# A deformable convolution's last three groups: two vertical taps per matmul; and a third x buffer in the wkv layer

## The chip, the cores and the metric

The kernel runs on one core of a Trainium2 chip. The metric is the time of one execution on the device in microseconds (us); lower is better. The core has five engines with their own instruction queues: PE (TensorE, matmuls, with its weight loads as PEld), DVE (VectorE), ACT (ScalarE), POOL (GpSimd) and SP (SyncE, which here only issues DMA transfers). They meet through semaphores.

## What is computed

Four residual layers on x, an array of (2, 192, 96, 96) floats, each on a group-normalised copy: layer 0 is a pair of deformable convolutions, layer 1 a 1 x 1 convolution with edge features, layer 2 a two-way RWKV recurrence ("wkv"), layer 3 a state space model. The change touches layers 0 and 2. All arithmetic is in 32-bit floats.

```python
# layer 0: twice (width and height branch), G = 10 groups of 18 channels, 9 taps
patches = val.reshape(Bx, C, KK, Hx, Wx)      # bilinear samples at learned offsets
out = jnp.einsum('bikhw,oik->bohw', patches, weight.reshape(Cout, Cin, KK))
# layer 2: per channel, forward and backward over the 9216 positions
no = jnp.maximum(o, u + kt); A = jnp.exp(o - no); Bw = jnp.exp(u + kt - no)
y = (A * p + Bw * vt) / (A * q + Bw)
no2 = jnp.maximum(w + o, kt)
A2 = jnp.exp(w + o - no2); B2 = jnp.exp(kt - no2)
carry = (A2 * p + B2 * vt, A2 * q + B2, no2)
```

## The kernel before

**Layer 0, near0 (L473 on).** It runs once for each of the two images; while image 0 runs, `reduce0` prepares image 1 in between (matmuls at L302, loads of `xt` at L285). An image has 79 tiles: 72 of 8 x 16 positions in 12 strips of six, and 7 on the right and lower edge. A tile passes three stages l = 0, 1, 2, each for up to four groups of channels. In a stage PE transposes the interpolation weights `sp` (L587; copied out by ACT L595 and DVE L593 as `st`), and `sample` multiplies them with the windows `xw` (L634). ACT copies the samples to `val` (L655). POOL makes the hats `h` (L541) and loads `xw` (L559), DVE the products `sp` (L571).

`gathered` (L661 on) then moves `val` with SP's DMAs, group by group, 18 lanes each, into two tiles that are laid out by channel: `main` for the first seven groups (126 lanes, both branches behind one another; L672, 14 transfers a tile) and `more` for groups 7, 8 and 9 (54 lanes from lane 0 for one branch, 54 from lane 64 for the other; L679, 12 transfers a tile). `val` has three buffers per half, `main` and `more` two.

`convolve` (L683 on) multiplies by the weights: for each of 3 blocks of 64 output channels, each of 9 taps and each branch (`cv`) one matmul, added into `pf` in PSUM at a place that is shifted by the tap. The two branches use different columns of PE. It is a generator in three parts, 26, 28 and 54 matmuls: `main` in two halves, then `more`. They run during the next tile's stages 0, 1 and 2, each after that stage's `sample`. At the end of a chunk of three tiles DVE adds `pf` to the row buffer `fa`, and every six tiles `done` writes a strip. PE, ACT and DVE keep the program's order here; POOL and SP are ordered by the scheduler. SP also reads the offsets `raw` (L504) three tiles ahead, writes `u_d` (L520), and in image 0 loads `xt`.

**Layer 2 (L1499 on).** 18 chunks of 512 positions by 3 lane groups, first forward, then backward: 108 steps, software pipelined by the loop at its end. `load(i + 6)` reads x for a new chunk (`xt`, L1661, two buffers), `key` and `value` or `gate` multiply it on PE (all L1605), `top` scans on DVE (L1716), `weighted` makes four exponentials on ACT, each in two instructions (L1731, L1733): `b`, `a`, `eb`, `ea`. `a` and `ea` of the backward half share two PSUM buffers called `e`. `sums` runs two scans (L1755) and two products on DVE; `own`, `ended`, `crossed` and `added` are on POOL; `logged` (L1800, L1801) makes a reciprocal `r` on ACT for `scaled` on DVE (L1813 on). `tail` normalises a chunk and writes it out (L1827 to L1893). All but SP keep the program's order.

Of the kernel before, what the change touches and what calls it, by code (L numbers as in the profile page):

```python
# [6 lines left out]
F32 = mybir.dt.float32  # L7
# [11 lines left out]
P = 128  # L19
CH = 96  # L20
CM, MH = 180, 90
G, CG, KK = 10, 18, 9
# [8 lines left out]
PS = 4  # L31
# [3 lines left out]
LT = P  # L35
# [3 lines left out]
XW = 104  # L39
OB, OA = 97, 291  # L40
MAIN = 7
CO = 64
NO = 3
FEW = 4
# [17 lines left out]
class Net:  # L62
# [283 lines left out]
    def near_constants(self, wn, at_d):  # L346

        nc, tc, ins = self.nc, self.tc, self.ins
        con = {}
# [95 lines left out]
        con["one"] = one  # L445

        wd = wn.tile([MAIN * CG, 2, KK, NO * CO], F32, name="wd")
        wl = wn.tile([P, KK, NO * CO], F32, name="wl")
        nc.gpsimd.memset(wl, 0.0)
        nc.gpsimd.memset(wd[:, :, :, CM:], 0.0)  # L450
        for cv in range(2):
            src = ins["w_dcn"][cv].rearrange("(g t c) o -> g c t o", g=G, t=KK)
            for g in range(G):
                at = g * CG if g < MAIN else cv * 64 + (g - MAIN) * CG
                nc.gpsimd.dma_start(
                    out=wd[at : at + CG, cv, :, :CM] if g < MAIN else wl[at : at + CG, :, :CM],
                    in_=src[g],
                )
        con["wd"], con["wl"] = wd, wl

        bo = wn.tile([P, NO], F32, name="bo")
# [13 lines left out]
    def near0(self, b, xp_d, o_d, u_d, f_d, sums, far, top, con, aside=None):  # L475
# [5 lines left out]
        with ExitStack() as ctx:  # L481
# [178 lines left out]
                        )  # L660
                return vals  # L661

            def gathered(main, more, l, vals, nh):

                for e in range(2):
                    val = vals[e].rearrange("p s r c -> p s (r c)")
                    for q in range(2):
                        g = 4 * l + (2 * q if l < 2 else 0) + e
                        for h in range(nh):
                            from_ = slice(h * 64 + q * 32, h * 64 + q * 32 + CG)  # L670
                            if g < MAIN:
                                nc.sync.dma_start(  # L672
                                    out=main[g * CG : (g + 1) * CG, h], in_=val[from_]
                                )
                                continue
                            for cv in range(2) if l < 2 else (q,):
                                lane = cv * 64 + (g - MAIN) * CG
                                s0 = cv * KK if l < 2 else 0
                                nc.sync.dma_start(  # L679
                                    out=more[lane : lane + CG, h], in_=val[from_, s0 : s0 + KK]  # L680
                                )

            def convolve(pf, main, more, kind, e, parts, first, last):  # L683

                nh, rows, columns = parts
                todo = [(m, t) for m in range(NO) for t in range(KK)]
                cut = len(todo) // 2
                for l, part in ((0, todo[:cut]), (0, todo[cut:]), (1, todo)):
                    for m, t in part:
                        ky, kx = 2 - t // 3, 2 - t % 3  # L690
                        y, x = ((ky, 16 * e + kx), (ky, 32 * e + kx), (32 * e + ky, kx))[kind]
                        for cv in range(2):
                            at = slice(cv * 64, cv * 64 + (G - MAIN) * CG) if l else slice(0, MAIN * CG)
                            wt = con["wl"][at, t] if l else con["wd"][:, cv, t]
                            if kind == 1:
                                to = pf[cv * CO : (cv + 1) * CO, m, y : y + rows, x : x + nh * columns]
                                to = to.rearrange("p r (h c) -> p h r c", h=nh)
                            else:
                                to = pf[cv * CO : (cv + 1) * CO, m, y : y + nh * rows, x : x + columns]
                                to = to.rearrange("p (h r) c -> p h r c", h=nh)  # L700
                            took = more[at, :, t] if l else main[:, :, cv * KK + t]
                            nc.tensor.matmul(  # L702
                                to,
                                wt[:, m * CO : (m + 1) * CO],
                                took.rearrange("p h (r c) -> p h r c", c=columns),
                                start=first and l == 0 and t == 0,
                                stop=last and l == 1 and t == KK - 1,
                                skip_group_check=True,
                                tile_position=(at.start, cv * CO),
                            )  # L710
                    yield

            def done(i, fa, ed):

# [28 lines left out]
            fa = s1.tile([P, 3, 10, W + 4], F32, name="fa")  # L743
            nc.gpsimd.memset(fa, 0.0)
            ed = s1.tile([P, 3, H + 4, 4], F32, name="ed")
            nt = STRIPS * 6
            def plan(kind, i, j):

# [104 lines left out]
            for k, (n, l) in enumerate(stages):  # L853
                chunk, e, tile = work[n]
                size, patches = tile[2:]
                kind = chunk[0]
                if l == 0:
                    if n + 1 < len(work):
                        xws[n + 1] = windows(work[n + 1][2][1])
                    where = wheres.get(n + 2, iter(()))  # L860
                    if n + 3 < len(work):
                        wheres[n + 3] = placed(n + 3)
                        next(wheres[n + 3])
                hat = iter(())
                if k + 3 < len(stages):
                    hat = hatted(k + 3)
                    hs[k + 3] = next(hat)
                two = k + 1 < len(stages) and stages[k + 1][1] < 2
                if k + 1 < len(stages):
                    sts[k + 1] = [turn(sps[turned])]  # L870
                    turned += 1
                    if l == 2:
                        next(where, None)
                    make(turned + 1)
                if l == 0:
                    main = sb.tile([MAIN * CG, 2 * KK * LT], F32, name="main")
                    more = sb.tile([P, KK * LT], F32, name="more")
                    parts = split(kind, size, patches)
                    half = parts[1] * parts[2]
                    main, more = (  # L880
                        v[:, : parts[0] * m * half].rearrange("p (h s n) -> p h s n", s=m, n=half)
                        for v, m in ((main, 2 * KK), (more, KK))
                    )
                vals = sample(sts.pop(k), xws[n], l, kind, parts, patches)
                gathered(main, more, l, vals, parts[0])
                next(hat, None)
                next(hat, None)
                next(conv, None)
                if l == 1:
                    next(steps, None)  # L890
                    next(steps, None)
                if two:
                    sts[k + 1].append(turn(sps[turned]))
                    turned += 1
                if l == 0:
                    next(steps, None)
                if l == 1:
                    us[n + 2] = next(where, None)
                if l == 2:
                    next(where, None)  # L900
                    next(conv, None)
                    conv = convolved(n, main, more)
# [592 lines left out]
    def layer2(self, x, out, stats):  # L1495
# [4 lines left out]
        T = 512  # L1500
# [5 lines left out]
        with ExitStack() as ctx:  # L1506
# [3 lines left out]
            s4 = ctx.enter_context(tc.tile_pool(name="l2t", bufs=4))  # L1510
            s1 = ctx.enter_context(tc.tile_pool(name="l2o", bufs=1))
            sy = ctx.enter_context(tc.tile_pool(name="l2y", bufs=2))
            pk = ctx.enter_context(tc.tile_pool(name="l2k", bufs=2, space=PSUM))
            pv = ctx.enter_context(tc.tile_pool(name="l2v", bufs=1, space=PSUM))
            pa = ctx.enter_context(tc.tile_pool(name="l2a", bufs=2, space=PSUM))
# [139 lines left out]
            def load(i):  # L1655
                back, c, g = seq[i]
                if g == 0:
                    xts[back, c] = []
                    for b in range(B):
                        xt = sb.tile([CH, 2, T], F32, name=f"xt{b}")  # L1660
                        nc.sync.dma_start(out=xt, in_=halves(x[b])[:, :, c * T : (c + 1) * T])  # L1661
                        xts[back, c].append(xt)

# [70 lines left out]
                got[i][name] = e  # L1734

            def weighted(i):
                if seq[i][0]:
                    weight(i, "b", sb, "b2", -1.0, w)
                    weight(i, "a", pa, "e", 1.0, ew)
                else:  # L1740
                    weight(i, "b", sb, "b2", -1.0, w)
                    weight(i, "a", pm, "pm", 1.0, ew)
                weight(i, "eb", sb, "eb", -1.0, nu)
                weight(i, "ea", pa, "e", 1.0, u)

            def times_v(i):
# [747 lines left out]
```

## Time and profile before

| | |
|---|---|
| three runs | 10516.57, 10526.15, 10529.94 us (median 10526.15) |
| the profiled execution | 10534.88 us |
| its span, first to last instruction | 10533.1 us |
| mean granted clock of TensorE | 0.909 |
| busy in the span | PE 9365.6, DVE 8257.2, POOL 7013.2, ACT 6008.3 us |
| layer 0's tile loop, image 0 and 1 | about 374 to 2700 and 2700 to 5275 us |
| layer 2's loop, forward and backward | about 6150 to 6465 and 6465 to 7200 us |
| `pf<-more,wl` and `pf<-main,wd` at L702 | 17064 records each, PE busy 958 and 962 us |
| SP's transfers `main<-val`, `more<-val` | 2198 and 1884 |

A line of the profile's timeline gives start, duration, engine, source line, operation, what is written from what, the shape, and the number of merged instructions; in brackets stands how long the engine had been idle before, and what released it. "SPq" is SP's queue of DMA issues: its time is that of the issuing, not of the transfer. A plain 32-bit matmul has two records.

### The profile page before, as it was taken

To read this page: it belongs to the slowest core of one execution; us is meant where nothing else is said; L and a number is where in the kernel's file an instruction comes from. 1 tells how busy PE (TensorE), PEld (TensorE's weight loads), DVE (VectorE), ACT (ScalarE), POOL (GpSimd) and SP (SyncE) were. 2 spreads that over 40 slices of the span, in tenths; PEclk is the share of its full clock that TensorE was granted. 3 is DMA by queue.
4 is the path that set the end of the run, shared out by engine and by line. 5 is a ranking of instruction groups with operands and counts; after the bars stand their busy time and mean duration, and the time that the engine had idled before them with its cause. 6 is when DMAs were issued, how large, how long until landed. Compare 5 with 4: busy or idle time off the path is not lost. (4 is left out here: it accounts for less than half of the span.)

```text
span 10533.1 us, 230262 instructions
## 1 busy us (share of the span) xinstructions
PE 9365.6 (89%) x92614; PEld 5530.4 (53%) x92614; DVE 8257.2 (78%) x8704; ACT 6008.3 (57%) x11216; POOL 7013.2 (67%) x5527
## 2 busy tenths in 40 slices
PE   4799999999989999999966776787999999999998
PEld 3588888888868888888822222222222222222222
DVE  4677777777677777777755788883999999999999
ACT  0366666666666676666600168663666666666664
POOL 1466766766555666666511258773888888888888
PEclk8899999999989999999978888886888888888887
DMA  8433434433323333333344344432777777777776
GB/s 146 90 93 95 97 96 95 97 96 95 78 68 89 93 90 91 89 93 90 80 128 127 109 153 150 123 120 72 170 172 170 172 171 172 173 170 171 172 169 148
DMA packets 601281, 1282.72 MB, mean 122 GB/s; under 512 B 238700, under 2 KB 321888, under 8 KB 543808
## 3 DMA queue, kind: packets, MB, share of 16 engines
q1 hardware_dynamic: 387560, 1081.12, 41.7%
q0 software_dynamic: 103808, 133.18, 5.7%
q10 hardware_dynamic: 108840, 53.57, 2.0%
q8 instruction: 739, 12.11, 0.5%
q14 instruction: 334, 2.74, 0.1%
HBM read 786.57 MB, written 231.25 MB: 97 GB/s over the span
## 5 line engine op out<-in xcount | busy, mean ns | idle before, releaser
L571 DVE TENSOR_TENSOR sp<-h 128x2304 f32<-128x2304 f32 x790 | 2162.2, 2769 | 25.7 <-ACT h L550 25.7
L2236 DVE TENSOR_TENSOR_SCAN h<-da,state,bu 128x512 f32<-128x512 f32 x1632 | 1959.5, 1262 | 238.2 <-ACT da L2226 231.9
L595 ACT COPY st<-pt 128x512 f32<-128x512 f32 (+1 forms) x2370 | 1218.7, 517 | 1310.3 <-PE pt L587 1241.3
L2203 POOL TENSOR_TENSOR bu<-bu,bs 128x2048 f32<-128x2048 f32 x432 | 1954.0, 4523 | 16.9 <-DMA bu<-ud 16.8
L593 DVE COPY st<-pt 128x512 f32<-128x512 f32 x1580 | 1062.0, 687 | 985.2 <-PE pt L587 968.3
L587 PE MATMUL pt<-ident,sp 128*128 128x128 f32 x14220 | 1679.4, 276 | 97.9 <-DVE sp L571 56.6
L541 POOL TENSOR_TENSOR h<-u,step 128x1152 f32<-128x1152 f32 (+1 forms) x474 | 1202.5, 2551 | 816.6 <-DVE u L514 464.0
L587 PEld LDWEIGHTS pt<-ident,sp 128*128 128x128 f32 x14220 | 1565.8, 142 | 185.7 <-issue 93.0
L559 POOL DMA_DIRECT2D xw<-xp_d x2500 | 1393.4, 632 | 142.2 <-PE pt L634 83.1
L2226 ACT ACTIVATE da<-da,nA 128x512 f32<-128x512 f32 x1728 | 1048.9, 662 | 657.8 <-PE da L2212 656.5
L634 PE MATMUL pt<-st,xw 64*32 64x288 f32 (+1 forms) x30000 | 1075.8, 367 | 77.0 <-ACT st L595 30.9
L655 ACT COPY val<-pt 128x288 f32<-128x288 f32 (+1 forms) x3132 | 986.1, 398 | 209.3 <-PE pt L634 205.5
L2212 PE MATMUL da<-dl,spread 32*128 32x512 f32 x3456 | 984.7, 692 | 15.3 <-DVE h L2236 7.5
L702 PE MATMUL pf<-more,wl 54*64 54x128 f32 (+1 forms) x17064 | 958.2, 268 | 10.9 <-DMA more<-val 10.2
L702 PEld LDWEIGHTS pf<-main,wd 126*64 126x64 f32 x17064 | 889.6, 137 | 140.7 <-issue 132.5
L702 PE MATMUL pf<-main,wd 126*64 126x128 f32 (+1 forms) x17064 | 962.1, 270 | 1.0 <-DMA main<-val 0.3
L702 PEld LDWEIGHTS pf<-more,wl 54*64 54x64 f32 x17064 | 920.4, 136 | 48.1 <-issue 34.7
L634 PEld LDWEIGHTS pt<-st,xw 64*32 64x32 f32 x30000 | 541.1, 106 | 483.2 <-ACT val L655 172.8
L2259 DVE TENSOR_TENSOR hc<-h,cc 128x1536 f32<-128x1536 f32 x432 | 747.1, 1729 | 0.0
L2104 PE MATMUL pe<-xn,sb_w_in 96*128 96x512 f32 x864 | 572.2, 797 | 113.1 <-ACT xi L2112 63.4
L2270 POOL TENSOR_TENSOR hp<-h,cs 128x512 f32<-128x512 f32 x432 | 550.2, 1274 | 163.7 <-PE da L2212 96.5
L2212 PEld LDWEIGHTS da<-dl,spread 32*128 32x128 f32 x3456 | 300.6, 193 | 667.1 <-DVE h L2236 433.6
(338 smaller groups left out, 12827.6 us busy)
## 6 DMA issues: line engine op xcount, KB each, us to landing
bu<-ud SPq DMA_DIRECT2D x432, 1024.0 KB
main<-val SPq DMA_DIRECT2D x2016, 81.0 KB
more<-val SPq DMA_DIRECT2D x1728, 40.5 KB
xw<-xp_d POOLq DMA_DIRECT2D x2500, 26.0 KB
xt<-x_d SPq DMA_DIRECT2D x108, 384.0 KB
half_d<-hv SPq DMA_DIRECT2D x54, 768.0 KB
hv<-half_d SPq DMA_DIRECT2D x54, 768.0 KB
u_d<-u SPq DMA_DIRECT2D x158, 180.0 KB
```

Of the source, the lines that this page charges most:

```text
L541: nc.gpsimd.tensor_tensor(hs, u[:, :, 8 * KK * l : 8 * KK * l + n].unsqueeze(3).to_broadcast([P, 2, n, WS]), con["step"].unsqueeze(1).unsq ...
L559: nc.gpsimd.dma_start(out=xw[e * WN : (e + 1) * WN, i], in_=xp_d[y : y + WS, x : x + WS, e * CM // 2 : e * CM // 2 + XW],)
L571: nc.vector.tensor_tensor(sp.rearrange("p s (y x) -> p s y x", x=WS), hy.unsqueeze(3).to_broadcast([P, n, WS, WS]), hx.unsqueeze(2).to_bro ...
L587: nc.tensor.transpose(pt[:, q], sp[:, 2 * (q0 + q) : 2 * (q0 + q) + 2].rearrange("p e w -> p (e w)"), self.ident,)
L593: nc.vector.tensor_copy(st[:, q0 : q0 + m], pt[:, :m])
L595: nc.scalar.copy(st[:, q0 : q0 + m], pt[:, :m])
L634: nc.tensor.matmul(pvs[e][lane : lane + 32, j * w : (j + 1) * w], xw[e * WN : (e + 1) * WN, win, g * CG : g * CG + 32], sts[pair][e * WN : ...
L702: nc.tensor.matmul(to, wt[:, m * CO : (m + 1) * CO], took.rearrange("p h (r c) -> p h r c", c=columns), start=first and l == 0 and t == 0, ...
L2203: nc.gpsimd.tensor_tensor(bu, bu, got[s]["bs"].unsqueeze(1).to_broadcast([P, 4, T]), ALU.mult)
L2212: nc.tensor.matmul(das[r], spread[at, v].rearrange("p n e -> p (n e)"), got[s]["dl"][at, i], start=True, stop=True, tile_position=(32 * r, 0),
L2226: nc.scalar.activation(da, da, AF.Exp, scale=nA[:, 4 * q + r : 4 * q + r + 1])
L2236: nc.vector.tensor_tensor_scan(h[:, r], got[s]["da", q][r], bu[:, r], init, ALU.mult, ALU.add)
```

## The change

In layer 0, `more` holds the samples of the last three groups so that one matmul of 118 lanes covers two of the three vertical taps: the lanes from 0 hold one tap, the lanes from 64 another one stored a row later, with zeros in the row that each lacks. That matmul reads one row more (9 x 16 = 144 columns in a full tile). The third vertical tap stays a matmul of 54 lanes. For each block of outputs come 6 shared matmuls, then 6 single ones: 36 in place of 54. `more` becomes two fixed tiles used in turn, with three slots of three taps, set to zero when the tile's shape changes; the weights `wl` get the same slots (18 loads in place of 6). Every transfer into `more` becomes two, with one run per tap: 24 in place of 12 in a full tile. In layer 2, `xt` comes from a pool of its own with three buffers, and the backward half makes `eb` before `a`.

```diff
@@ gathered
-    lane = cv * 64 + (g - MAIN) * CG
+    lane = (g - MAIN) * CG
     s0 = cv * KK if l < 2 else 0
+    taps = val[from_, s0 : s0 + KK].rearrange("p (a t) n -> p a t n", a=3)
+    to = h * apart
+    put, took = (2, 2) if cv else (slice(0, 2), slice(1, 3))
     nc.sync.dma_start(
-        out=more[lane : lane + CG, h], in_=val[from_, s0 : s0 + KK]
+        out=more[lane : lane + CG, put, :, to : to + n],
+        in_=taps[:, took],
+    )
+    lane, to = lane + 64, to + columns
+    put, took = (slice(1, 3), slice(0, 2)) if cv else (0, 0)
+    nc.sync.dma_start(
+        out=more[lane : lane + CG, put, :, to : to + n],
+        in_=taps[:, took],
     )
@@ convolve
-    for l, part in ((0, todo[:cut]), (0, todo[cut:]), (1, todo)):
+    for part in (todo[:cut], todo[cut:]):
...
+    for m in range(NO):
+        for one in range(2):
+            for t in range(3):
+                for cv in range(2):
+                    at = 64 * cv * one
+                    lanes = slice(at, at + REST if one else 64 + REST)
+                    slot = 1 if one else 2 * cv
...
+                    nc.tensor.matmul(
+                        place(cv, m, (2 * cv if one else 1 - cv), 2 - t, 1 - one),
+                        con["wl"][lanes, slot, t, m * CO : (m + 1) * CO],
+                        took,
+                        start=False,
+                        stop=last and one == 1 and t == 2,
+                        skip_group_check=True,
+                        tile_position=(at, cv * CO),
+                    )
+    yield
@@ near0
+    mores = [s1.tile([P, 3, 3, LW], F32, name=f"more{i}") for i in range(2)]
+    shapes = [None, None]
...
-    more = sb.tile([P, KK * LT], F32, name="more")
+    more = mores[n % 2]
...
+    if shapes[n % 2] != (kind, parts):
+        shapes[n % 2] = (kind, parts)
+        nc.gpsimd.memset(more, 0.0)
@@ layer2
+    sx = ctx.enter_context(tc.tile_pool(name="l2x", bufs=3))
...
-    xt = sb.tile([CH, 2, T], F32, name=f"xt{b}")
+    xt = sx.tile([CH, 2, T], F32, name=f"xt{b}")
@@ weighted
+    weight(i, "b", sb, "b2", -1.0, w)
     if seq[i][0]:
-        weight(i, "b", sb, "b2", -1.0, w)
+        weight(i, "eb", sb, "eb", -1.0, nu)
         weight(i, "a", pa, "e", 1.0, ew)
     else:
-        weight(i, "b", sb, "b2", -1.0, w)
         weight(i, "a", pm, "pm", 1.0, ew)
-    weight(i, "eb", sb, "eb", -1.0, nu)
+        weight(i, "eb", sb, "eb", -1.0, nu)
     weight(i, "ea", pa, "e", 1.0, u)
```

More of the change, by code (lines that the diff above doesn't have):

```diff
@@ L41 @@
 MAIN = 7
+REST = (G - MAIN) * CG
+LW = (PS * 2 + 1) * 16
 CO = 64
@@ L447, in near_constants @@
         wd = wn.tile([MAIN * CG, 2, KK, NO * CO], F32, name="wd")
-        wl = wn.tile([P, KK, NO * CO], F32, name="wl")
+        wl = wn.tile([P, 3, 3, NO * CO], F32, name="wl")
         nc.gpsimd.memset(wl, 0.0)
@@ L453, in near_constants @@
             for g in range(G):
[L454 to L458, printed above, removed]
+                if g < MAIN:
+                    at = g * CG
+                    nc.gpsimd.dma_start(out=wd[at : at + CG, cv, :, :CM], in_=src[g])
+                    continue
+                low = slice((g - MAIN) * CG, (g - MAIN + 1) * CG)
+                high = slice(64 + low.start, 64 + low.stop)
+                for lanes, slot, a in (
+                    ((high, 1, 0), (high, 2, 1), (low, 2, 2))
+                    if cv
+                    else ((high, 0, 0), (low, 0, 1), (low, 1, 2))
+                ):
+                    nc.gpsimd.dma_start(
+                        out=wl[lanes, slot, :, :CM], in_=src[g][:, 3 * a : 3 * a + 3]
+                    )
         con["wd"], con["wl"] = wd, wl
@@ L661, in sample, with gathered @@
                 return vals
-            def gathered(main, more, l, vals, nh):
+            def gathered(main, more, l, vals, kind, parts):
+                nh, rows, columns = parts
+                n = rows * columns
+                apart = n + columns if kind == 1 else n
                 for e in range(2):
@@ L676, in gathered @@
                             for cv in range(2) if l < 2 else (q,):
-                                lane = cv * 64 + (g - MAIN) * CG
+                                lane = (g - MAIN) * CG
                                 s0 = cv * KK if l < 2 else 0
-                                nc.sync.dma_start(
-                                    out=more[lane : lane + CG, h], in_=val[from_, s0 : s0 + KK]
+                                taps = val[from_, s0 : s0 + KK].rearrange(
+                                    "p (a t) n -> p a t n", a=3
+                                )
+                                to = h * apart
+                                put, took = (2, 2) if cv else (slice(0, 2), slice(1, 3))
+                                nc.sync.dma_start(
+                                    out=more[lane : lane + CG, put, :, to : to + n],
+                                    in_=taps[:, took],
+                                )
+                                lane, to = lane + 64, to + columns
[3 more added lines that the diff above has]
+                                    in_=taps[:, took],
                                 )
@@ L687, in convolve, with place @@
                 cut = len(todo) // 2
-                for l, part in ((0, todo[:cut]), (0, todo[cut:]), (1, todo)):
+                def place(cv, m, ky, kx, extra):
+                    y, x = ((ky, 16 * e + kx), (ky, 32 * e + kx), (32 * e + ky, kx))[kind]
+                    if kind == 1:
+                        to = pf[cv * CO : (cv + 1) * CO, m, y : y + rows + extra, x : x + nh * columns]
+                        return to.rearrange("p r (h c) -> p h r c", h=nh)
+                    to = pf[cv * CO : (cv + 1) * CO, m, y : y + nh * rows + extra, x : x + columns]
+                    return to if extra else to.rearrange("p (h r) c -> p h r c", h=nh)
@@ L689, in convolve @@
+                for part in (todo[:cut], todo[cut:]):
                     for m, t in part:
-                        ky, kx = 2 - t // 3, 2 - t % 3
-                        y, x = ((ky, 16 * e + kx), (ky, 32 * e + kx), (32 * e + ky, kx))[kind]
                         for cv in range(2):
[L693 to L707, printed above, removed]
@@ L708, in convolve @@
+                            nc.tensor.matmul(
+                                place(cv, m, 2 - t // 3, 2 - t % 3, 0),
+                                con["wd"][:, cv, t, m * CO : (m + 1) * CO],
+                                main[:, :, cv * KK + t].rearrange("p h (r c) -> p h r c", c=columns),
+                                start=first and t == 0,
+                                stop=False,
                                 skip_group_check=True,
-                                tile_position=(at.start, cv * CO),
+                                tile_position=(0, cv * CO),
@@ L710, in convolve @@
                             )
                     yield
+                for m in range(NO):
[5 more added lines that the diff above has]
+                                slot = 1 if one else 2 * cv
+                                took = more[lanes, slot, t]
+                                if kind == 1:
+                                    took = took[:, : nh * (rows + 1) * columns].rearrange(
+                                        "p (h r c) -> p h r c", h=nh, c=columns
+                                    )
+                                    if one:
+                                        took = took[:, :, cv : cv + rows]
+                                elif one:
+                                    took = took[:, cv * columns : (cv + nh * rows) * columns]
+                                    took = took.rearrange("p (h r c) -> p h r c", h=nh, c=columns)
+                                else:
+                                    took = took[:, : (nh * rows + 1) * columns].rearrange(
+                                        "p (r c) -> p r c", c=columns
+                                    )
+                                nc.tensor.matmul(
[6 more added lines that the diff above has]
+                                    tile_position=(at, cv * CO),
+                                )
@@ L876, in near0 @@
                     main = sb.tile([MAIN * CG, 2 * KK * LT], F32, name="main")
-                    more = sb.tile([P, KK * LT], F32, name="more")
+                    more = mores[n % 2]
                     parts = split(kind, size, patches)
                     half = parts[1] * parts[2]
-                    main, more = (
-                        v[:, : parts[0] * m * half].rearrange("p (h s n) -> p h s n", s=m, n=half)
-                        for v, m in ((main, 2 * KK), (more, KK))
-                    )
+                    main = main[:, : parts[0] * 2 * KK * half].rearrange(
+                        "p (h s n) -> p h s n", s=2 * KK, n=half
+                    )
+                    if shapes[n % 2] != (kind, parts):
+                        shapes[n % 2] = (kind, parts)
+                        nc.gpsimd.memset(more, 0.0)
                 vals = sample(sts.pop(k), xws[n], l, kind, parts, patches)
-                gathered(main, more, l, vals, parts[0])
+                gathered(main, more, l, vals, kind, parts)
                 next(hat, None)
```

## The prediction

> **What bounds the kernel now.** I read the page's slices first, then busy time by stretch, then the timelines of TensorE (PE) and of SP's queue over one tile, then the waits. The change touches two stages: the tile loop of layer 0 (374 to 5275 us; image 0 to about 2700, image 1 after it) and the wkv layer (6150 to 7200 us). In the busy-time answer the columns are stretch, length, PE, PEld, DVE, ACT, POOL (each with its count), granted clock, DMA share, GB/s:
>
> ```profile
> 4401.16:4430.67 29.51, 29.38 (x506) 24.84 (x499) 22.07 (x21) 20.66 (x44) 16.55 (x19) 1.00 0.37 86
> 6520.00:7140.00 620.00, 488.94 (x1178) 138.93 (x1180) 519.98 (x677) 396.65 (x699) 456.16 (x351) 0.87 0.39 116
> ```
>
> In one tile of layer 0 PE works 29.38 of 29.51 us at full clock, DVE 22.07, ACT 20.66, POOL 16.55: PE sets the pace. In the backward half of the wkv layer DVE is busiest (520 of 620 us), with 100 us idle. PE's timeline of that tile:
>
> ```profile
> 4401.16 6.16 PE L702 MATMUL pf<-more,wl 54*64 54x128 f32 x108
> 4407.25 4.15 PE L587 MATMUL pt<-ident,sp 128*128 128x128 f32 x36
> ...
> 4414.58 3.06 PE L702 MATMUL pf<-main,wd 126*64 126x128 f32 x52
> 4417.57 4.15 PE L587 MATMUL pt<-ident,sp 128*128 128x128 f32 x36
> ...
> 4424.15 3.28 PE L702 MATMUL pf<-main,wd 126*64 126x128 f32 x56
> 4427.36 2.18 PE L587 MATMUL pt<-ident,sp 128*128 128x128 f32 x18
> ```
>
> The block that the change rewrites (three last groups, `more`) takes 4407.25 - 4401.16 = 6.09 us for 108 records, two records per matmul. The same tile on SP's queue:
>
> ```profile
> 4402.84 0.41 SPq L520 DMA_DIRECT2D u_d<-u  x1
> 4403.35 6.05 SPq L679 DMA_DIRECT2D more<-val  x8
> 4409.44 0.67 SPq L504 DMA_DIRECT2D raw<-o_d  x1
> 4415.14 14.07 SPq L672 DMA_DIRECT2D main<-val  x14
> 4429.31 2.93 SPq L679 DMA_DIRECT2D more<-val  x4
> ```
>
> This is the second resource. Eight issues take 6.05 us and the next begins 0.04 later: 0.76 us each. A tile has 14 + 12 = 26 of them, 19.8 us, plus `u_d` 0.51 and `raw` 0.74 with their gaps: 21.0 us of issuing in a 29.5 us tile, the rest waits for ACT's `val`.
>
> **Layer 0, PE.** The `more` block goes from 27 pairs of 128 columns to 9 pairs of 144 columns (three groups, two vertical taps in 118 lanes) and 9 pairs of 128. Records: 108 become 36 + 36. Price: 52 `main` records start to start take 2.99 us and 56 take 3.21, so 0.055 each with 0.13 us per block; the `more` block gives 6.09 - 108 x 0.055 = 0.15. For columns: the same block with 64 columns takes 3.46 us (5235.14 to 5238.60), so a column is worth (6.09 - 3.46) / 108 / 64 = 0.00038 us and a 144-column record 0.061. The new order alternates the two kinds three times, six blocks instead of one. New time: 36 x 0.061 + 36 x 0.055 + 6 x 0.14 = 5.02 us; saved 1.07 us a tile. If alternating costs nothing it is 1.77; if each of the five added boundaries cost 0.35 us it is nothing (PEld's idle ahead of such blocks is 0.17 to 0.47 us). I take 0.14, because four boundaries of this tile show it. The Trainium skill, TensorEngine Tiling (Array Packing), Key Properties, says that changing the tiling mode drains the engine, which speaks against this interleaving; it names no price, and the 0.13 to 0.15 us per block above is what a drain can have cost here.
>
> Six tiles (one strip) take 178.6 us in image 1 (block starts 3623.30 to 3801.87) and 195.0 in image 0 (898.98 plus 37.82, 31.91, 30.99, 32.34, 30.96, 30.96), where reducing the other image rides along. A strip's saving is 6.4 us. Image 0's tiles also have small PE waits for DVE's `sp`, which will take some back: I take 12 strips x 6.4 = 77 down to 60 us.
>
> **Layer 0, SP's queue.** Every `more` transfer becomes two, of 54 and 108 runs of 256 bytes instead of 18 runs of 2304 (full tile): 38 issues of this kind a tile. At 0.76: 28.9 + 0.51 + 0.74 = 30.1 us; image 0 adds one `xt` load (0.47 + 0.07), 30.7. By strip: 180.8 us in image 1 against PE's 178.6 - 6.4 = 172.2; 184.0 in image 0 against 195.0 - 6.4 = 188.6. So **image 1 becomes bound by SP's issuing**: 180.8 - 178.6 = +2.2 a strip, x 12 = +26 us. Image 0 keeps its gain. Behind a late SP stand `raw` (read three tiles ahead), `u_d`, and the tiles' `main`, which PE needs one stage later; `main` lands some 14 us ahead of use now, so the lag inside a strip (5 x 0.7 us in image 0) is covered. DVE's pause at a strip's end (a 33.70 us tile) then costs PE nothing, since PE is ahead of SP.
>
> The unknown is what one new issue costs. The trace has no three-level transfer on 18 lanes. From below: `main` with 4608-byte runs and `more` with 2304 or 1152 all have the same minimum of 0.697 us, so size does not count; `wx` into strided SBUF in three levels (L1984 to L1986) took 0.43, 0.49, 0.49 beside 0.43 for its plain neighbours; `ud<-du` in three levels has a minimum of 0.308 against 0.327 for plain `u_d`. From above: where the two sides are shaped differently (`cs<-br`, L2150) the minimum is 0.514 against 0.305 for a plain `yo`, +0.2. I take +0, being nearest to `wx`, which has the same form. Each 0.01 us costs 24 x 0.01 x 72 = 17 us in image 1, and the same in image 0 once its 6 us a strip of room are used, at about +0.04. Below zero I see no reason.
>
> The many small runs also load the DMA engines:
>
> ```profile
> 133.89 0.40 SPq L424 DMA_DIRECT2D at_d<-where  x1
> 134.76 21.80 SPq L285 DMA_DIRECT2D xt<-in_x  x1
> ```
>
> `at_d` has 128 x 79 = 10112 runs of 16 bytes; the issue behind it was held 21.8 us, that is 21.8 / (10112 / 16) = 0.034 us a run and engine. A tile's 1944 runs are 122 an engine if spread evenly, 4.1 us at 0.034 and 22 us at the 0.181 us that a packet of q1, 2.8 KB on average, took (41.7% of 16 x 10533 us over 387560 packets). With today's mean share of 0.37 (11 us) that is 15 to 33 us of 30: room by the first, none by the second. I take the first, small runs on the same queue. The Trainium skill, DMA: Bandwidth & Descriptors, Specifications, asks for at least 512 bytes per transfer and says that smaller ones are read, modified and written; that speaks against this change, and by it the runs would lie nearer the upper price and the sum nearer the third rival below.
>
> POOL starts with 32 weight loads instead of 20. The 20 took 3.36 to 43.98 us, 2.0 each, so +24 us and two memsets of 1.2; POOL then idles 34.3 us until 89.4, which covers them. Without cover it would be 27 us. Twelve later memsets of 1.2 us lie in POOL's 30% idle time.
>
> **The wkv layer.** Only the backward half (54 steps, 18 chunks) changes its order. One step:
>
> ```profile
> 6792.67 0.60 ACT L1733 ACTIVATE e<-t 128x512 f32<-128x512 f32 x1 [2.73 <-DVE opq L1755]
> 6793.20 0.71 ACT L1731 ACTIVATE t<-z,nu 128x512 f32<-128x512 f32 x1
> 6794.00 0.63 ACT L1733 ACTIVATE eb<-t 128x512 f32<-128x512 f32 x1
> ...
> 6797.62 0.69 DVE L1813 TENSOR_TENSOR nd<-nd,r 128x512 f32<-128x512 f32 x1 [0.64 <-ACT r L1801]
> ...
> 6803.57 3.75 PE L1605 MATMUL k<-xt,wk 96*128 96x512 f32 x4 [2.65 <-DMA xt<-x_d]
> ```
>
> ACT idles until DVE's scan frees the buffer of weight `a`; then comes `eb`, and at the end `r`, for which DVE waits. With `eb` ahead its 1.34 us run in that idle time. DVE's waits for `r` are 69.3 us in 48 times: per chunk 0.65, 1.14 and 2.5 us, of which 0.65 + 1.14 + 1.34 = 3.13 go, x 16 chunks = 50 us. The wait before a chunk's first `k` (46.7 us in 13 times) goes with the third x buffer, since in the changed order SP loads one chunk later at the same place; it reaches DVE through the late tail matmuls as the rest of the 2.5 us and as `yo`'s wait (20.4 us): up to 2.3 x 16 = 37 us. Together 50 to 87; DVE idles 100 in all, and PE (489) and POOL (456) then follow close behind, so I take 65, from 25 if POOL takes over to 90. Nothing new is queued on ACT: `a` waits on the same scan as before. The forward half is ACT's own (304 of 315 us), so no gain.
>
> **Sum.** -60 + 26 - 65 = -99 us on this execution's 10534.9 (span 10533.1): 10436. Its run was 9 us above the median of 10526.15; I leave that in the range.
>
> **Rivals.**
> - Forecast (0.55): as above, 10436; its own range 10350 to 10510.
> - SP's queue decides, slower (0.30): a three-level issue costs +0.1 us. -99 + 173 + 173 - 72 (image 0's room of 0.042) = +175: 10710. The deciding point is +0.05, where the sum is zero; at +0.2 it is 11050. For: 72% of a tile is issuing already, and `cs<-br`. Against: `wx`.
> - The DMA engines hold SP (0.05): at the 33 us above, 2.9 us a tile over SP's 30.1 in image 1 and 1.6 over image 0's 31.4, x 72 = +324: 10760. It decides where a run costs over (30.1 - 11) / 122 = 0.16 us.
> - Layer 0 gives nothing at all, because the added boundaries eat the block's saving or SP stops at +0.03 to +0.05, and the wkv layer keeps 40 (0.10): 10495 to 10540.
>
> **Numbers.** A measurement of this kernel tells about 0.2%, 21 us. Faster 0.57, same 0.08, slower 0.35. The range takes the forecast with all lower bounds (image 0 at 77, free boundaries up to its SP floor, the wkv layer at 90: about 10350) and the slower case to +0.1: 10350 to 10710.
>
> **What would show it.** The `more` block near 5 us in six pieces. Issues at L698 and L704 of 0.70 us: right; 0.75 or more: the rival. In image 1 PE idle about 2 us a tile ahead of `main` matmuls on DMA, strips of 181 us; in image 0 strips near 190. ACT's wait for the scan in front of `a`, DVE's wait for `r` nearly gone, no `k` waiting for `xt`. I am wrong if SP's strips exceed 187 us, or if the backward half stays above 600 us for the same 16 chunks.

## The result and the profile after

The changed kernel takes **10859.33 us** (median of 4 runs, 10850.16 to 10862.73) against 10521.36 of the kernel before in the same comparison (10515.56 to 10529.94): ratio 1.0319, 95% interval 1.0301 to 1.0337. It is slower by 338 us. The forecast was 10436, and its range ended at 10710. The profiled execution has a span of 10861.0 us; the mean granted clock is 0.895, where before had 0.909.

Line numbers move: SP's transfers into `more` are now L698 (first) and L704 (second), into `main` L686; the `main` matmuls are L726, the `more` matmuls L757, the transposes L598, `u_d` L531 and `raw` L515.

SP's queue over one tile of image 1 (start, duration, line, operation, tensors, count):

```profile
4423.86 0.79 SPq L698 DMA_DIRECT2D more<-val  x1
4424.69 0.79 SPq L704 DMA_DIRECT2D more<-val  x1
4425.52 0.65 SPq L515 DMA_DIRECT2D raw<-o_d  x1
4426.27 10.68 SPq L686 DMA_DIRECT2D main<-val  x14
4437.05 0.82 SPq L698 DMA_DIRECT2D more<-val  x1
4437.91 0.80 SPq L704 DMA_DIRECT2D more<-val  x1
...
4443.78 0.41 SPq L531 DMA_DIRECT2D u_d<-u  x1
4444.30 0.81 SPq L698 DMA_DIRECT2D more<-val  x1
...
4456.85 0.79 SPq L704 DMA_DIRECT2D more<-val  x1
4457.69 0.65 SPq L515 DMA_DIRECT2D raw<-o_d  x1
4458.44 11.03 SPq L686 DMA_DIRECT2D main<-val  x14
```

There is no hole in this queue. One starts where the last ended: 0.83 us from start to start for each of the 24 transfers into `more`, 10.78 / 14 = 0.77 for `main`, 0.52 and 0.75 for `u_d` and `raw`. That adds up to 31.97 us, and `raw` comes back after 32.17. In the kernel before the `main` issues were spread over 14.07 us, since they waited for `val`. SP's own waits show the same. The two longest of before over 3200 to 5200 us, then the two longest of after over 3200 to 5400 (engine, line, what it waited for: us in total, times, longest):

```profile
SPq L672 <- ACT val L655: 586.8, 134, 8.0
SPq L672 <- ACT st L595: 39.1, 59, 1.6
```

```profile
SPq L686 <- ACT st L606: 35.0, 66, 0.9
SPq L698 <- ACT st L606: 26.4, 46, 0.8
```

The room of 587 us is gone; nothing that is left in the list lasts longer than 1.1 us. PE over the same tile:

```profile
4423.45 0.43 PE L757 MATMUL pf<-more,wl 118*64 118x144 f32 x2 [0.20 <-DMA more<-val]
4427.01 6.64 PE L757 MATMUL pf<-more,wl 118*64 118x144 f32 x70 [3.14 <-DMA more<-val]
4433.59 4.15 PE L598 MATMUL pt<-ident,sp 128*128 128x128 f32 x36
...
4456.35 0.46 PE L757 MATMUL pf<-more,wl 118*64 118x144 f32 x2
4459.15 5.10 PE L757 MATMUL pf<-more,wl 118*64 118x144 f32 x70 [2.34 <-DMA more<-val]
```

PE starts the `more` block, finds that SP's last transfers have not landed, and stands for 2 to 3 us: 130.5 us in 57 waits over 3200 to 5400 us. In before, the waits for `more` come to 0.5 us in all over 3200 to 5200 us. The two blocks differ in length because the granted clock was 0.74 in the first and 1.00 in the second. Over 3200 to 5400 us its mean is 0.96, where before has 1.00 over 3200 to 5200, so PE works a little slower too; but SP's queue is full without a hole, and a plain issue takes it as long as before, so this does not set the pace.

The price of an issue is read from the answer on a source line (duration in ns, least / median / most):

```profile
L698 SPq DMA_DIRECT2D more<-val x1884: 765/787/1625, 399.2 to 5631.5; - x189
L704 SPq DMA_DIRECT2D more<-val x1884: 757/787/1686, 400.1 to 5632.4; - x189
L686 SPq DMA_DIRECT2D main<-val x2198: 697/698/1601, 387.9 to 5612.2; - x200
```

A transfer into the new three-level shape (lane, tap, position: one run for each lane and tap) costs 0.787 us, a plain one 0.698, as before (0.702). L698 writes 108 runs and L704 54 for one branch, and the reverse for the other; in full tiles the median is 0.787 for both numbers, so the number of runs makes no difference.

**Where the 338 us are.** The issues of `u_d`, one a tile (79 an image), serve as a clock of layer 0. Between the first and the last of them before takes 4842.8 us (362.5 to 5205.3) and after 5198.4 (357.5 to 5555.9), +356. Of the 66 tiles in the middle of each image, image 0 goes from 2133.6 to 2207.2 us (+74) and image 1 from 1974.5 to 2162.4 (+188); the first and last tiles of the images and the passage between them carry the other 94. Among them are the small tiles of the image's edge, most of which have as many transfers with smaller matmuls. Behind the last `u_d`, SP's transfers go on for 76 us, where before had 60. In mean pitch (over 66 tiles in image 0 and 64 in image 1, here and below): **32.33 to 33.44 us a tile in image 0, 29.94 to 32.78 in image 1.** The loop of the wkv layer takes 38 us less (994.1 to 955.9 us from its first weight to its last scan, both halves), nearly all of it in the backward half.

### The profile page after: what moved, and what is told of

The parts are those of the page before. It is cut to its first block, busy times and chain, and to the rows that moved or that the text cites. A ratio compares the mean times of both kernels' runs of the same rounds, so it can differ in the third digit from the quotient of the medians.

```text
span 10861.0 us, 221908 instructions
## 1 busy us (share of the span) xinstructions
PE 9395.0 (87%) x86926; PEld 5386.5 (50%) x86926; DVE 8250.2 (76%) x8704; ACT 6021.1 (55%) x11216; POOL 6970.8 (64%) x5553
## 2 busy tenths in 40 slices
DMA packets 889703, 1282.25 MB, mean 118 GB/s; under 512 B 560840, under 2 KB 641436, under 8 KB 832252
## 3 DMA queue, kind: packets, MB, share of 16 engines
q1 hardware_dynamic: 675812, 1081.19, 40.5%
## 5 line engine op out<-in xcount | busy, mean ns | idle before, releaser
L552 POOL TENSOR_TENSOR h<-u,step 128x1152 f32<-128x1152 f32 (+1 forms) x474 | 1131.2, 2402 | 1021.1 <-DVE u L525 518.4
L598 PE MATMUL pt<-ident,sp 128*128 128x128 f32 x14220 | 1678.6, 276 | 69.8 <-DVE sp L582 35.8
L598 PEld LDWEIGHTS pt<-ident,sp 128*128 128x128 f32 x14220 | 1571.0, 142 | 151.2 <-issue 92.0
L757 PE MATMUL pf<-more,wl 54*64 54x128 f32 (+4 forms) x11376 | 946.6, 307 | 246.0 <-DMA more<-val 241.9
L726 PE MATMUL pf<-main,wd 126*64 126x128 f32 (+1 forms) x17064 | 1003.7, 277 | 98.7 <-DMA main<-val 52.3
L726 PEld LDWEIGHTS pf<-main,wd 126*64 126x64 f32 x17064 | 932.0, 142 | 247.8 <-issue 180.2
L757 PEld LDWEIGHTS pf<-more,wl 118*64 118x64 f32 (+1 forms) x11376 | 721.6, 150 | 470.7 <-issue 429.2
```

What stands on the lines that cost most here:

```text
L552: nc.gpsimd.tensor_tensor(hs, u[:, :, 8 * KK * l : 8 * KK * l + n].unsqueeze(3).to_broadcast([P, 2, n, WS]), con["step"].unsqueeze(1).unsq ...
L598: nc.tensor.transpose(pt[:, q], sp[:, 2 * (q0 + q) : 2 * (q0 + q) + 2].rearrange("p e w -> p (e w)"), self.ident,)
L726: nc.tensor.matmul(place(cv, m, 2 - t // 3, 2 - t % 3, 0), con["wd"][:, cv, t, m * CO : (m + 1) * CO], main[:, :, cv * KK + t].rearrange(" ...
L757: nc.tensor.matmul(place(cv, m, (2 * cv if one else 1 - cv), 2 - t, 1 - one), con["wl"][lanes, slot, t, m * CO : (m + 1) * CO], took, star ...
```

## The experiments

The theory after the result (S): the SP queue bounds layer 0, by the price of the three-level form and by the doubled number of issues; PE's saving is hidden behind it. The rivals: short runs fill the DMA engines (D), or PE's shared matmuls lose time themselves (P).

**1. The two layers apart.** Only layer 0's part of the change:

> The layer 0 part of the change alone, the wkv layer as before. Theory (SP's queue is full of issues in layer 0): the whole loss is here and a little more, since the wkv part gives about 38 us back (its loop runs from the first weight to the last scan in 955.9 us after, 994.1 before): 10521 + 376 = about 10897 us. Rival (the two parts disturb each other through memory placement or order): the loss is clearly less than 338 + 20 us.

Only the wkv part:

> The wkv part alone, layer 0 as before. Theory: about 38 us faster, 10483 us. If the parts do not add up with the run of layer 0 alone to +338 us within 15 us, they interact.

Layer 0 alone: 10908.48 us, 1.0366 [1.0348, 1.0383], pitch 33.43 and 32.85. The wkv part alone: **10481.94 us, 0.9955 [0.9938, 0.9972]**, against 10525.78. +383 and -44 make +339: the parts add up. The wkv part or one of its halves alone is all that beats the kernel before.

**2. The halves of the wkv part.** Only the third x buffer (`xt` from a pool of three):

> Only the third x buffer in the wkv layer. Theory A (the late x load cost mostly through the tail's late matmuls): 10 to 25 us faster, the wait of k for xt gone, DVE's wait for r down by its long cases. Rival B (the x load is hidden behind DVE, only the order of eb matters): within 5 us of before.

Only the weight sooner:

```
     if seq[i][0]:
+        weight(i, "eb", sb, "eb", -1.0, nu)
         weight(i, "a", pa, "e", 1.0, ew)
     else:
         weight(i, "a", pm, "pm", 1.0, ew)
-    weight(i, "eb", sb, "eb", -1.0, nu)
+        weight(i, "eb", sb, "eb", -1.0, nu)
```

> Only eb ahead of a in the backward half. Theory A: 20 to 30 us faster (DVE's wait for r, 69 us before, loses its 0.65 and 1.14 us cases, the cases behind a late x stay). Rival B: nearly all of the 38 us. In both DVE's new wait for the tail's matmuls (yo for pm, 20 us before, 43 after) shows.

The buffer alone gives 10511.05 us, 0.9986 [0.9977, 0.9996]; the weight alone 10503.58, 0.9977 [0.9967, 0.9988]: -15 and -22, both as expected under A; both at once give -44. The waits over 6500 to 7200 us (total, times, longest), first of before, then with the weight alone, then with the wkv part whole:

```profile
DVE nd L1813 <- ACT r L1801: 75.4, 51, 7.8
PE k L1605 <- DMA xt<-x_d: 46.7, 13, 7.0
DVE yo L1883 <- PE pm L1873: 37.9, 18, 6.0
```

```profile
PE k L1605 <- DMA xt<-x_d: 54.9, 15, 6.3
DVE nd L1813 <- ACT r L1801: 47.2, 25, 6.5
```

```profile
DVE yo L1884 <- PE pm L1874: 57.7, 31, 7.0
DVE nd L1814 <- ACT r L1802: 7.8, 11, 1.6
```

With the weight alone the waits for `r` that are left are half as many but longer on average: mostly one of about 2 us or more per chunk, soon after `k`'s wait for `xt`. With both parts the wait for `r` is nearly gone, and DVE then waits for PE's late tail (`yo`) 20 us more.

**3. More issues without the form; the form without more issues.** The kernel before, with each transfer into `more` cut in two plain ones:

```
+    for t0, t1 in ((0, 5), (5, KK)):
         nc.sync.dma_start(
-            out=more[lane : lane + CG, h], in_=val[from_, s0 : s0 + KK]
+            out=more[lane : lane + CG, h, t0:t1], in_=val[from_, s0 + t0 : s0 + t1],
         )
```

> The kernel before, but each transfer into more is cut in two (taps 0 to 4 and 5 to 8), both plain, in runs of 1280 and 1024 bytes; nothing else changes. Theory S (SP's issuing sets the tile time): 38 issues of 0.76 us plus 1.25 us are 30.1 us, with the 0.9 us of irregular issues that the changed kernel shows 31.0: image 1 goes from 29.9 to about 31.0 us a tile, image 0 stays near 32.3; in all +60 to +110 us, 10580 to 10630. Rival R (the many 256-byte runs hold the DMA engines): no change, as there are few and long runs.

The kernel before, with as many transfers as ever, but each in three levels: `more` holds its taps at a pitch of LT + 16, so that every transfer is cut into nine runs of 256 bytes a lane (162 runs, 1944 a tile, as in the change):

```
-    out=more[lane : lane + CG, h], in_=val[from_, s0 : s0 + KK]
+    out=more[lane : lane + CG, :, h * half : h * half + half],
+    in_=val[from_, s0 : s0 + KK],
```

> The kernel before, but more is laid out tap by tap with a gap behind each, so each of its 12 transfers a tile is three-level with nine runs of 256 bytes: 1944 short runs a tile as in the changed kernel, with half its issues. Theory S: an issue takes 0.79 us as in the changed kernel (price of the form), SP is at 21 + 12 x 0.08 = 22 us a tile, below PE: no change, within 20 us of before. Rival R: the loss of the changed kernel is back, +200 us or more.

The first takes 10629.86 us, 1.0097 [1.008, 1.0114], pitch 32.11 and 30.62: the upper end of what S gave. The second takes 10526.18, 0.9996 [0.9987, 1.0006], pitch 32.04 and 29.98, as S had it. Its issues and SP's longest wait over 3200 to 5200 us:

```profile
L679 SPq DMA_DIRECT2D more<-val x1884: 761/787/1937, 399.4 to 5248.8; - x189
```

```profile
SPq L672 <- ACT val L655: 530.2, 134, 7.9
```

This parts the causes. The price of 0.787 belongs to the form, and 162 runs cost no more than 54. Twelve such issues take 57 us out of SP's wait and nothing out of the clock, so as long as SP has room the price is free, and 1944 short runs a tile leave the mean pitch where it was: D falls. Nor does the number alone explain it: 38 plain issues a tile cost 98 us, not 383.

**4. Both together, without the new matmuls.** The layout of the last kernel, every transfer cut into two three-level ones, with the matmuls of before:

```
+    for t0, t1 in ((0, 6), (6, KK)):
         nc.sync.dma_start(
-            out=more[lane : lane + CG, :, h * half : h * half + half],
-            in_=val[from_, s0 : s0 + KK],
+            out=more[lane : lane + CG, t0:t1, h * half : h * half + half],
+            in_=val[from_, s0 + t0 : s0 + t1],
         )
```

> The kernel before with its 54-lane matmuls, wkv layer as before, but with the changed kernel's issues: each transfer into more is cut in two three-level ones (six and three runs of 256 bytes). SP gets the changed kernel's 24 + 14 issues. Theory S: layer 0's tiles take the changed kernel's 33.4 and 32.8 us although PE's work is unchanged: 10880 to 10920, as the run of the layer 0 part alone (10908). Rival (part of the loss comes from the new matmul blocks or from how they wait): below 10850.

It takes 10886.06 us, 1.0352 [1.0335, 1.037]: +366 with not one matmul changed, and the pitch of 33.27 and 32.66 is that of the change (33.43 and 32.85 for layer 0 alone). PE in one of its tiles:

```profile
4408.00 6.18 PE L708 MATMUL pf<-more,wl 54*64 54x128 f32 x108
...
4418.19 2.65 PE L634 MATMUL pt<-st,xw 64*32 64x288 f32 x64
4422.87 4.73 PE L708 MATMUL pf<-main,wd 126*64 126x128 f32 x52 [2.03 <-DMA main<-val]
...
4440.64 6.33 PE L708 MATMUL pf<-more,wl 54*64 54x128 f32 x108
```

The old block of 108 records is there, and from one to the next there are 32.64 us, as in the change. SP's own waits over 3200 to 5400 us are 1.2 us at most (1.1 in the change). So **SP's issuing alone brings back 366 of layer 0's 383 us**, and whatever PE saves is hidden behind it. That settles S for all but the 17 us, which no run takes apart.

**5. Can SP be relieved?** All twelve second transfers of a tile on POOL (`nc.gpsimd` in place of `nc.sync` at L704):

> The whole change, but the second transfer of each pair is issued from POOL: SP has 14 + 12 issues a tile (22 us), POOL 12 more (about 0.6 to 0.75 us each, 8 us on top of 16.6 of 29.5). Theory S: layer 0 gets PE's gain after all, 27.9 to 29 us a tile in image 1 and 31.4 in image 0, with the wkv part's 38 us: 10330 to 10420. Rival R: the short runs are still there, so the loss stays, above 10700. Rival P (the six alternating blocks of matmuls cost what they save): near 10480. If POOL becomes late with hats and windows: up to 10500.

The eight transfers of stage 1 on ACT's queue (`queue = nc.scalar if l == 1 else nc.sync`):

> The whole change, but the eight transfers into more of stage 1 are issued from ACT's queue, right after ACT wrote val: SP has 25.4 us of issuing a tile, ACT 20.7 + 8 x 0.8 = 27.1 us. Theory S: SP no longer sets the pace, image 1 between 28 and 30 us a tile: 10350 to 10500. Rival R: above 10700.

Both miss. POOL: 10767.0 us, 1.0224 [1.0207, 1.0241], pitch 34.92 and 30.74; most tiles of image 1 take 28 to 29.5 us, but one in each strip 36 to 39, and in image 0, where POOL also writes out what `reduce0` makes, 40 to 46. In image 0 (700 to 2700 us) ACT waits for POOL's hats once a strip:

```profile
ACT h L559 <- POOL h L552: 127.4, 11, 15.3
```

ACT: 11251.46 us, 1.0686 [1.0668, 1.0704], pitch 35.89 and 35.49. Its ACT over one stage, then PE's wait for ACT over 3200 to 5400 us:

```profile
4403.69 0.80 ACTq L699 DMA_DIRECT2D more<-val  x1
4404.52 0.80 ACTq L705 DMA_DIRECT2D more<-val  x1
...
4409.55 0.85 ACTq L705 DMA_DIRECT2D more<-val  x1
4410.44 1.16 ACT L559 ACTIVATE h<-h 128x1152 f32<-128x1152 f32 x1 [6.78 <-DMA more<-val]
```

```profile
PE pt L645 <- ACT st L606: 237.6, 62, 6.7
```

Eight issues stop ACT for 6.8 us. The hats (`h`) and the copies `st` that stand behind them are late, and PE waits for `st` about once a tile. Issuing takes an engine's working time here.

**6. Less on POOL, fewer blocks.** Only the eight second transfers of stage 2 on POOL:

> The whole change, but only stage 2's eight second transfers are issued from POOL, which had to wait for val in stage 1 and did not in stage 2. SP: 14 x 0.77 + 16 x 0.83 + 1.25 + 0.9 irregular = 26.2 us a tile, below PE. Theory S: PE sets the pace again; its more block takes 5.48 us in the run with twelve on POOL (6.09 before), so 0.6 us a tile on 144 tiles, 88 us, and the wkv part's 44: 10400; up to 10480 if POOL, with 5 us more a tile, is late at strip ends. Rival R (short runs): above 10700.

The same with all shared matmuls first and the single ones after (`for one` outside `for m`: two blocks instead of six):

> As the run with eight transfers on POOL, but the shared matmuls of all three output blocks come first and the single ones after them: two blocks instead of six. Theory P (each change between 118-lane and 54-lane matmuls costs PE (5.48 - 36 x 0.061 - 36 x 0.055) / 6 = 0.22 us): the block falls to about 4.6 us, another 0.88 us a tile, 10280 to 10350. Rival (the boundaries cost nothing and single records are slower than estimated): the block stays at 5.48, the time within 20 us of that run.

The first takes 10688.64 us, 1.0164 [1.0147, 1.0181], pitch 33.85 and 30.62, and misses 10400 to 10480; the second 10638.88, 1.0117 [1.0101, 1.0134], pitch 33.98 and 30.05. In both SP waits for `val` again (262.6 us at L686 in the second). The `more` block, now without a wait for data, of the first and then of the second kernel:

```profile
4421.62 5.54 PE L758 MATMUL pf<-more,wl 118*64 118x144 f32 x72 [0.15 <-issue]
4427.09 4.15 PE L598 MATMUL pt<-ident,sp 128*128 128x128 f32 x36
```

```profile
4394.07 4.95 PE L758 MATMUL pf<-more,wl 118*64 118x144 f32 x72 [0.15 <-issue]
4398.95 1.31 PE L598 MATMUL pt<-ident,sp 128*128 128x128 f32 x10
```

From start to start 5.47 and 4.88 us; four boundaries fewer are worth 0.59, **0.15 us each**. All these blocks ran at a granted clock of 1.00. PE's saving exists (6.09 before), so P falls, but each strip still has a late tile: 35 to 41 us in image 1, 36 to 46 in image 0. POOL there, in the second kernel:

```profile
4432.58 4.41 POOL L784 TENSOR_SCALAR f<-fa,bo 128x768 f32<-128x768 f32 x2 [1.65 <-DVE fa L774]
4437.57 2.19 POOL L793 DMA_DIRECT2D f_d<-f  x4 [0.58 <-POOL f L784]
4443.57 2.21 POOL L784 TENSOR_SCALAR f<-fa,bo 128x768 f32<-128x768 f32 x1 [3.81 <-DMA f_d<-f]
...
4447.46 2.93 POOL L839 COPY fa<-fa 128x600 f32<-128x600 f32 x1
...
4450.93 2.12 POOL L840 MEMSET fa<- 128x2400 f32 x1
```

At a strip's end POOL has the output's bias, its stores and the shift of `fa`, and it begins the next `h` only at 4456.80.

**7. The strip's end taken from POOL.** POOL's eight transfers in image 1 alone, two blocks, the bias on DVE, its stores on SP in image 1:

> Here the second transfers of stage 2 go to POOL in image 1 alone, the order is that of two blocks, the three additions of the bias at a strip's end are done by DVE instead of POOL, and in image 1 SP issues their six stores. If POOL's lateness at the strip ends is what kept the matmul block's saving from the clock (a mean tile pitch of 30.05 us in image 1 with a tile of 36 to 38 us in each strip and 27 to 29 us otherwise), that tile falls to 30 to 33 us, image 1's mean to 28.5 to 29.3 (before: 29.94), the first time that layer 0 gains anything; image 0 stays bound by SP near 33.4, so the whole is 10460 to 10530 us. If the saving is hidden by something else, DVE or ACT late at the strip's end, that tile stays over 35 us, image 1's mean at 30 or more, and the whole at 10580 or more.

It takes 10599.78 us, 1.0064 [1.0047, 1.0081], pitch 33.40 and 29.63. Image 1 is for the first time under before's 29.94, but the tile of 37 to 39 us stays. The forecast of 10460 to 10530 misses; what came is near its alternative, DVE late at the strip's end, except for the mean of 29.63:

```profile
4428.73 0.62 DVE L784 TENSOR_SCALAR f<-fa,bo 128x768 f32<-128x768 f32 x1 [3.28 <-DMA f_d<-f]
...
4429.49 0.68 POOL L839 COPY fa<-fa 128x600 f32<-128x600 f32 x1 [4.42 <-DVE f L784]
...
4430.47 5.01 DVE L582 TENSOR_TENSOR sp<-h 128x2304 f32<-128x2304 f32 x2
...
4433.16 6.35 PE L598 MATMUL pt<-ident,sp 128*128 128x128 f32 x36 [5.42 <-DVE sp L582]
```

Now DVE stands at the third bias for a buffer whose store is still under way, and `sp` and PE come late behind it. The wait for `f_d` has gone from one engine to another; a third buffer for `f` was not tried. Whether layer 0 can gain with the strip's end mended stays open.

## Why the prediction was wrong

It named the right resource and lost the sign by one price; the size had further causes. The row from which it took the price, in before (duration in ns, least / median / most):

```profile
L1984 SPq DMA_DIRECT2D wx<-in_w_x x1: 434/434/434, 7209.4 to 7209.4; - x1
L1985 SPq DMA_DIRECT2D wx<-in_w_x x1: 488/488/488, 7209.9 to 7209.9; - x1
L1986 SPq DMA_DIRECT2D wx<-in_w_x x1: 487/487/487, 7210.4 to 7210.4; - x1
```

- **The step that failed: "I take +0"** for what a three-level issue costs over 0.76 us. The issue takes 0.787 instead of 0.70 us, 0.83 from start to start, hence +0.07 (the result's lines and experiment 3). The prediction set its own deciding point at +0.05 and had the mechanism as a rival at +0.1. The row that it took, `wx`, does not even say +0. Two of its three issues are 0.05 to 0.06 us over the plain 0.43 ahead of them, which is the deciding point itself. The row also has 128 lanes and reads from HBM, and the price of the new form was the term on which the sum hung. At +0.07 the 24 issues cost 1.68 us a tile. By the prediction's own rule (17 us for each 0.01 us and image, less 72 us of room) that turns -99 into about +70, and not into +338; the rest is in the items below.
- **Also in that step: a floor without unevenness.** The sum of SP's issues for image 1 was 30.1 us a tile, and the kernel with 38 plain issues (experiment 3), to which the +0 applies, has 30.62. So even at +0 the -99 would not have come: with that kernel's +98, the prediction's -60 for image 0 and the measured -44, about nothing is left (an estimate). In the change the regular issues make 31.97, and the mean is 32.78: 0.8 us more, from single issues of up to 1.6 us and gaps of up to 0.4 us between issues. As long as SP waits for `val`, such an issue costs nothing; in a queue that sets the pace each counts. Of image 1's 2.65 us over 30.13 (180.8 / 6), 1.68 are the price, 0.14 `main` at 0.77 and 0.83 the unevenness.
- **"Image 0 keeps its gain" (-60)**: the same error. At 33.44 SP is over PE there too, and the gain turns into +1.11 a tile. The images' ends, which were not in the sum, add 94 us.
- **PE's block**: 5.47 us, not 5.02. The boundary was right (0.15 for 0.14); the records were not: (4.88 - 2 x 0.15) / 72 = 0.064 us each on average in place of the 0.058 that 36 x 0.061 and 36 x 0.055 make. The saving is 0.62 us a tile and not 1.07. It reached the clock in no tile in which SP set the pace.
- **The wkv layer**: mechanism right, size off, -44 instead of -65. `r`'s wait goes from 75.4 to 7.8 us and `k`'s 46.7 are gone, but `yo`'s wait was to go as well, and it rose from 37.9 to 57.7: what is late next is PE's tail.
- **DMA engines (0.05) and POOL's longer start**: right. Packets under 512 bytes rose from 238700 to 560840, and the share of q1 fell from 41.7 to 40.5% in a longer span, about the same time in all. The rule on 512 bytes that the prediction cites did not decide here (experiment 3). The first `u_d` is at 357.5 us, 5 earlier than before, so the added weight loads were covered.
- The signs that were to show an error did: strips of 6 x 32.78 = 197 us where over 187 was to mean wrong, and issues at 0.787 where 0.75 was the rival. PE's wait of about 2 us a tile is ahead of `more`, though, and not mainly of `main`: the last issue before the block is the late one.

## What to carry to other kernels

Count the issues of each queue per step of the loop and multiply them by the price of their own form; a queue that shows waits for a producer has that much room and no more, and a change that adds issues must pay for them out of it. Where the price of a new form decides the sign, a row of another shape is no price, least of all one whose own spread is as large as the deciding point: measure it alone, as the form at the old number of issues (free) and the old form at the new number (+98 us) did here, and expect the two to cost far more together (+366), since the first part of what is added only fills the room. Moving issues to another engine makes them work of that engine: look where it is already late, here at the end of each strip.

## What the runs showed of the hardware

- Issuing an SBUF to SBUF transfer on 18 lanes costs 0.70 us on SP whether it is a whole transfer into `main` or half a one into `more` (experiment 3: 697/698 ns for four or five taps). With a three-level side it is 0.787, for 54, 108 or 162 runs alike. ACT takes 0.80 for the same, POOL 0.60 (4.83 us for eight).
- The Trainium skill, DMA: Bandwidth & Descriptors, Issuing engines are not separate DMA queues, says that issuing from several engines only saves the sequencer's time to initiate, usually small beside the transfer. Here that time was the bound: 38 issues fill a tile of 32 us at a DMA share of 0.33 (3200 to 5400 us).
- The same page, Why small descriptors are slow (HBM only), exempts transfers between SBUF and SBUF from the penalty on small runs. Experiment 3 agrees: with 1944 runs of 256 bytes a tile the time is 0.9996 [0.9987, 1.0006] of before, and q1's share 42.8% against 41.7.
